# A transformer block with a depthwise convolution on one core: load order, where the residual sums are kept, an unpadded ring of pixels, and another folded tap

## The chip, the cores and the metric

The kernel runs on one core of a Trainium2 chip. The metric is the device time of one execution in microseconds; three runs of the kernel before gave 4190.55, 4192.3 and 4199.95 us, so the median is 4192.3 us.

The core's engines work side by side, each through its own queue in order: TensorE (PE) multiplies matrices, VectorE (DVE) and ScalarE (ACT) work element by element, GpSimd (POOL) does small arithmetic and issues the DMAs that add to their destination, SyncE (SP) issues plain loads and stores. Sixteen DMA engines carry all transfers.

## The reference

The input x has 16 images of 128 channels and 96 x 96 pixels, all float32. Per image the block computes, with every weight an input:

```python
xn1 = layernorm(x)                       # over the 128 channels of a pixel
q, k, v = xn1 @ wq.T, xn1 @ wk.T, xn1 @ wv.T   # 8 heads of 16 channels
attn = softmax(l2norm(q) l2norm(k)^T * 16**-0.5)   # 16 x 16 per head: sums over all 9216 pixels
x = x + (attn v) @ wp.T
xn2 = layernorm(x)
h1 = w_in xn2                            # 128 -> 512 channels
h2 = depthwise 3x3 convolution of h1, zero padding
x = x + w_out gelu(h2)                   # 512 -> 128 channels
```

The attention mixes channels, not pixels, so that per image it comes down to one 128 x 128 matrix and a bias (`mats`), which need the Gram matrix of all normalised pixels of that image.

## The kernel before, in words

**Tiling.** An image is cut into 8 bands of 12 rows (`BR`), a band into 3 units of 4 rows (`UR`, 384 pixels). Channels lie on the 128 partitions. There are 128 bands in all.

**First pass, norm a.** A band of x is loaded (L547). PE transposes 128 pixels at a time (L610), DVE takes mean and variance (L617), POOL computes the variance plus epsilon (L624) and its power -1/2 (L628), ACT scales the transposed pixels (L664), PE adds them to the Gram matrix (L678) and transposes them back (L715), and ACT copies them into the padded pixel tiles `xn` (L721).

**Attention.** Some twenty short steps on several engines turn the Gram matrix into `mats` (L779 to L875).

**Second pass, norm b.** PE multiplies a unit of normalised pixels by `mats` (L567). Either DVE adds the result to the x that is still in SBUF (L573; image 0, its first `XB_BUFS` = 6 bands), or ACT writes it with the bias into a buffer `xb` (L576) and a DMA of POOL adds x from DRAM (L579). The sum stays in that buffer. It is normalised as before (L610, L617, L624, L628, L632, L668, L715) and ACT writes the result over the same place of `xn` (L719), with a row more to the neighbouring part at a part's edge (L725).

**FFN.** The 512 hidden channels are 4 chunks. A *job* is one chunk of one band on the vector path: PE computes the hidden rows from `xn` (L900), ACT copies them to a padded buffer `h1` (L905), and two of 14 rows are kept for the next band by a copy of ACT (`halo`, L896). The tap at the corner, number 0, is folded into the hidden weights (`units`, L487), so that its product is the hidden value itself. Of the other eight taps DVE does six (L918, each multiplies and adds 1152 values per partition). ACT does two as products (L913), and two DMAs of POOL add them, one product to the other and the sum to `h3` (L922). ACT takes the GELU (L926). Chunk 3 of 62 of the 128 bands goes through PE instead: nine matmuls a unit with `w_in` and the tap multiplied together (`comp`, L968), and ACT's GELU (L974). That makes 450 jobs. PE multiplies `h3` by `w_out` (L991), ACT copies the result out (L1003), a DMA of POOL adds it to `xb` in SBUF (L1006), and SP stores `xb` to the output (L1010). In the last two bands DVE does that addition (L998).

**Pixels.** `xn` is six tiles of 24 rows with a row above and below and a zero column between rows (97 values a row); `window` takes shifted views of them. POOL zeroes the outer rows anew for each image (L407).

**Order.** Nothing is ordered by hand. `Plan` (L56) takes every operation with its engine, an assumed duration, a place (a job's number plus the offset of its kind in `AT`), what it reads and writes, and the pools of buffers; it then plays the engines through in time, each taking its ready operation with the lowest place, and the program is written in that order. Engines then run their queues in order and wait by semaphores. The assumed durations (`T_VARIANCE`, `T_POWER`, `T_ADD`, `t_dve`, ...) and `AT` therefore decide what stands behind what.

Of the kernel before, what the change touches and what calls it, by code (L numbers as in the profile page):

```python
# [26 lines left out]
THIRD, THIRD_OF, THIRD_CHUNK = (), 3, 1  # L27
PART, Z_PARTS = 24, 6
QT, QB = 4, 1
H_BANKS = 4  # L30
X1_BUFS, XB_BUFS, PR_BUFS, H3_BUFS, ZT_BUFS = 2, 6, 5, 10, 3
ADD_OF, ADD_BY_DMA = 1, (0,)
IN_TURN = ("tr", "h3", "pr", "xb", "x1")
AT = dict(
    load_w=10.25, weights=-46.8, zeros=-149.95, load_a=-129.7, forth_a=-2.85, stats_a=-6.55, variance_a=297.7,
    power_a=264.8, scaled_a=76.85, gram=-0.15, back_a=-106.5, place_a=51.75, attention=-125.2, mix=-20.25,
    residual=220.6, mixed=-149.95, add_x=-343.4, forth_b=0.85, stats_b=-219.5, variance_b=53.7, power_b=-244.15,
    shift_b=-78.6, scaled_b=4.05, back_b=-14.85, place_b=-112.4, evicted=4.9, add_out=-1.85, halo=191.1,
    hidden=2.75, kept=2.7, products=1, add_last=-73.7, tap=9.7, add_first=-58.05, gelu=173.1, conv=2.7,
    conv_gelu=8.75, out=6.1, add=-35.75, store=139.7, mix_0=-63.25, residual_0=414.1, mixed_0=-164.45,  # L40
    add_x_0=-281.3, gram_0=-43.8, forth_a_0=-74.3, forth_b_0=1.05, stats_a_0=-30.2, stats_b_0=-254.35,
    scaled_a_0=-88.5, scaled_b_0=171.2, back_a_0=-144.35, back_b_0=-18.9, place_a_0=-142.05, place_b_0=49.7,
    shift_b_0=-116.3, late=-68.9,
)
STEP = dict(scaled=0.3, hidden=0.1, products=0.5, tap=0.166, conv=1.6, conv_tap=0.03, out=0.8, out_part=0.05)
SLACK = 300
# [3 lines left out]
T_WEIGHTS = 12000  # L50
T_VARIANCE = 420
T_POWER = 1000
T_ADD, T_MOVE = 3100, 1800


class Plan:  # L56
# [7 lines left out]
    def __init__(self, **pools):  # L64
        self.free = {p: list(range(n)) for p, n in pools.items()}
        self.slot = {}
        self.ops, self.writer, self.readers, self.users = [], {}, {}, {}
        self.dma = 0.0
        self.two = 0.0

    def op(self, engine, ns, place, work, reads, writes, result, own=None, dma=0, two=False):
# [27 lines left out]
        self.ops.append((engine, ns, place, work, list(needs), new, result, own or result, dma, two))  # L99

    def order(self):
# [38 lines left out]
        def dispatch(engine, time):  # L140
# [19 lines left out]
            if o[8]:  # L160
                self.dma = max(time + ns + WAIT[engine], self.dma) + o[8]
                result = own = self.dma + result - time
            elif engine == "POOL":
                rest = self.two - time
                ns, result = (ns, result) if rest <= 0 else (rest + ns - 143, rest + result - 143)
                own = result
            if o[9]:
                self.two = time + ns + 35
# [42 lines left out]
def tile_restormer_block(  # L211
# [35 lines left out]
    UPP, PARTS = PART // UR, H // PART  # L247
    D = C // HEADS
    assert PE_CHUNK == NCH - 1 and BR * W >= 8 * P and QT % 2 == 0 and NU * TPU % (QB * QT) == 0 and C == P and UT % P == 0 and H % PART == 0 and PART % BR == 0 and NCH == 4
# [11 lines left out]

    xbs, x1s = {}, {}
# [12 lines left out]
    def column(v, name):  # L275
        t = const.tile([P, 1], F32, name=name)
        nc.scalar.dma_start(out=t, in_=v.rearrange("(c o) -> c o", o=1))
        return t

    w1, b1 = column(ln1_w, "w1"), column(ln1_b, "b1")  # L280
    w2, b2 = column(ln2_w, "w2"), column(ln2_b, "b2")

    wv_sb = const.tile([P, P], F32, name="wv_sb")
    nc.scalar.dma_start(out=wv_sb, in_=wv)
# [4 lines left out]
    nc.scalar.dma_start(out=dw, in_=w_dw.rearrange("(n p) o kh kw -> p n (o kh kw)", p=P))  # L289

# [13 lines left out]
    xns = [pad.tile([P, (PART + 2) * WP + 2], F32, name=f"xn{k}") for k in range(Z_PARTS)]  # L304
# [21 lines left out]
    def part_of(i, r):  # L326

        return (i * PARTS + r // PART) % Z_PARTS, r % PART

    def interior(i, u):  # L330
        k, r = part_of(i, u * UR)
        return window(xns[k], r + 1, UR, 1)

    def z_unit(i, u):
        k, r = part_of(i, u * UR)
        return ("z", k, r // UR)
# [8 lines left out]
    grams, mats, h3s, staged, outs = {}, {}, {}, {}, {}  # L345
# [12 lines left out]
    def z_units(k, r0, r1):  # L358

        return [("z", k, u) for u in range((r0 + UR - 1) // UR - 1, (r1 - 2) // UR + 1)]  # L360

# [4 lines left out]
    def t_dve(n):  # L366
        return 100 + 1.067 * n

    def t_act(n, scalars=0):
        return 95 + 93 * scalars + 0.832 * n  # L370

    def t_copy(n):
        return 40 + 0.832 * n
# [4 lines left out]
    def dve(ns, p, f, r, w, two=False):  # L378
        op("DVE", ns, p, f, r, w, ns + 120 + SLACK, ns + 120, two=two)

# [9 lines left out]
    def zeros(p):  # L390


        def around(t, r):
            nc.gpsimd.memset(t[:, : r * WP].rearrange("p (r w) -> p r w", w=WP)[:, :, :1], 0.0)
            nc.gpsimd.memset(t[:, r * WP :], 0.0)
# [3 lines left out]
        for t, r in [(t, PART + 2) for t in xns[:PARTS]] + [(t, BR + 2) for t in h1s] + [(t, PART + 2) for t in xns[PARTS:]]:  # L399
            op("POOL", 1000, at("zeros", p), lambda t=t, r=r: around(t, r), [], [("w", "in")], 1200)  # L400

    def ends(p, i):

        for r, at_, u in ((0, 0, -1), (H - 1, PART + 1, UPP)):
            k = part_of(i, r)[0]
            row = window(xns[k], at_, 1, 1)
            op("POOL", 400, at("zeros", p), lambda row=row: nc.gpsimd.memset(row, 0.0), [], [("z", k, u)], 600)  # L407

    def weights(p):

        mine = [("h3", ("weights", k)) for k in range(2)]
        v, names = staged, iter(range(99))

        def loads():
            a, b = (h3p.tile([P, BR * W], F32, tag="h3", name=f"weights_{k}") for k in range(2))
            v["win"] = a[:, :HID].rearrange("p (n c) -> p n c", c=P)
            v["wout"], v["wp"] = a[:, HID : 2 * HID], a[:, 2 * HID : 2 * HID + P]
            v["wqk"], v["wqkT"] = b[:, : 2 * P], b[:, 2 * P : 4 * P]
            v["wt"] = b[:, 4 * P : 8 * P].rearrange("p (t c) -> p t c", c=P)
            v["centre"], v["w1centre"], v["wvT"] = b[:, 8 * P : 9 * P], b[:, :P], b[:, P : 2 * P]  # L420
            nc.scalar.dma_start(out=v["wqk"][:, :P], in_=wq)
            nc.scalar.dma_start(out=v["wqk"][:, P:], in_=wk)
            nc.scalar.dma_start(out=v["wp"], in_=wp)
            nc.scalar.dma_start(out=v["win"], in_=w_in.rearrange("(n p) c kh kw -> p n (c kh kw)", p=P))
            nc.scalar.dma_start(out=v["wout"], in_=w_out.rearrange("c j kh kw -> c (j kh kw)"))

        def transposed(kind, parts, kept, gives):
# [10 lines left out]
            pe(440, at(kind, p), forth, mine, [h])  # L438
# [46 lines left out]
        def units():  # L485

            w0 = dw[:, :, 0]  # L487
# [12 lines left out]
        op("ACT", 400, at("load_w", p), loads, [], mine, T_WEIGHTS, dma=2 * T_MOVE)  # L500
        dve(1400, at("weights", p), units, [], [("w", "in")])
        dve(400, at("weights", p), shifts, [], [("w", "in"), ("w", "conv"), ("w", "shift")])
        transposed(
            "weights", lambda: [v["wqk"][:, :P], v["wqk"][:, P:], v["wp"], wv_sb], keep_qkp, ["qk"]
# [29 lines left out]
    def x_key(i, b, second):  # L534

        return "xb" if second or i == 0 and b < XB_BUFS else "x1"
# [14 lines left out]
    def norm(i, second, place_of):  # L551
# [8 lines left out]
        def x2(s, u):  # L560
# [19 lines left out]

            pm = ("h", (name, u))
            ins = [z_unit(i, u), ("m", i)]
            if loaded:
                pe(t_mm(UT), at("mix", s, i), mix, [*ins, xtok(u)], [pm])
                dve(t_dve(UT), at("residual", s, i), residual, [pm], [xtok(u)])
                return
            pe(t_mm(UT), at("mix", s, i), mix, ins, [pm, xtok(u)])
            act(t_act(UT, 1) - 43, at("mixed", s, i), mixed, [pm], [xtok(u)])
            if u % UPB == UPB - 1:
                xb = [xtok(b * UPB + k) for k in range(UPB)]  # L590
                add(at("add_x", s, i), add_x, [], xb)

        def pixels(s, m):
# [88 lines left out]

            trs, bt = [(key_, (name, q)) for q in qs], ("batch", (name, m))
# [5 lines left out]
            op("POOL", T_VARIANCE, at("variance" + ab, s), variance, [], [bt], T_VARIANCE + 33 + SLACK)  # L689
            op("POOL", T_POWER, at("power" + ab, s), power, [], [bt], T_POWER + 33 + SLACK)  # L690
# [16 lines left out]
        def channels(s, u):  # L707
# [15 lines left out]
            def place_row(k, r, row):  # L723
                to = window(xns[k], r, 1, 1)
                nc.scalar.activation(to, rows(d["pB"])[:, row : row + 1, :], AF.Identity, bias=b2)  # L725

            copies = []
            if second and u % UPP == 0 and u > 0:
                copies.append((part_of(i, u * UR - 1)[0], PART + 1, 0, UPP))
            if second and u % UPP == UPP - 1 and u < NU - 1:  # L730
                copies.append((part_of(i, (u + 1) * UR)[0], 0, UR - 1, -1))

# [4 lines left out]
            for k, r, row, of in copies:  # L737
                act(225, at("place" + ab, s, i), lambda k=k, r=r, row=row: place_row(k, r, row), [pb, ("w", "shift")], [("z", k, of)])


        for u in range(0, NU if not second else 0, UPB):
            load(at("load_a", place_of(u * TPU)), i, u // UPB)
# [139 lines left out]
    def conv_job(j, g, n):  # L882

        i, b = divmod(g, NB)
        kz, r0 = part_of(i, b * BR)
# [204 lines left out]
```

## Time and profile before

| what | before |
|---|---|
| runs | 4190.55, 4192.3, 4199.95 us |
| span of the profiled execution, first to last instruction | 4197.8 us (2.15 us under the slowest of the runs, 5.5 us over their median) |
| PE busy | 4120.2 us (98%) |
| DVE busy | 4089.8 us (97%) |
| ACT busy | 3697.8 us (88%) |
| POOL busy | 2606.6 us (62%) |
| bytes moved by DMA | 831.16 MB, mean 198 GB/s |
| DMA queue of POOL (adds) / of SP (loads, stores) | 83.3% / 9.8% of the 16 engines' time |

Busy times are of the instructions as recorded, which overlap at their ends: for the pace of an engine that works without a gap, the distance from one start to the next is read from the chain of waits. A row of the windows gives, for a stretch of time, each engine's busy microseconds and, at its end, the granted clock of PE, the share of the DMA engines' time and the GB/s. A row of the groups gives line, engine, operation, output and inputs, count, busy time, mean ns of one, and after the bar the engine's idle time just before them and what ended it.

### The profile page before, as it was taken

How to read it: one execution, taken by the hardware profiler on the slowest of the kernel's cores; microseconds unless marked ns; L12 is line 12 of the kernel's file. 1: busy time of each engine (PE TensorE's matmuls, PEld its weight loads, DVE VectorE, ACT ScalarE, POOL GpSimd, SP SyncE). 2: the span in 40 equal slices, each digit the busy share in tenths (PEclk: the TensorE clock that was granted, in tenths of full speed). 3: DMA queues.
4: the chain of work that ended last, by engine and by line, in shares of the span. 5: the costliest groups of instructions: out<-in, count | busy, mean ns of one | idle time of the engine just before them, and what ended most of it. 6: DMA issues, size and time to landing. Idle time of an engine off the chain costs nothing.

```text
span 4197.8 us, 52159 instructions
## 1 busy us (share of the span) xinstructions
PE 4120.2 (98%) x17265; PEld 2648.1 (63%) x17265; DVE 4089.8 (97%) x4450; ACT 3697.8 (88%) x7232; POOL 2606.6 (62%) x2397
## 2 busy tenths in 40 slices
PE   8999999999999999999999999999999999999999
PEld 6666666666666666656666666666666666665555
DVE  6999999999999999999999999999999999999998
ACT  5899988999899888889899989998899888999885
POOL 4757666565666757767576565666656666675442
PEclk9999999999999999999999999999999999999999
DMA  3899999999999999999999999999999999999997
GB/s 91 178 195 213 194 215 196 198 203 204 205 206 202 209 193 205 198 211 202 195 210 205 204 203 199 210 199 210 200 204 208 194 212 200 201 203 191 196 190 167
DMA packets 204797, 831.16 MB, mean 198 GB/s; under 512 B 23664, under 2 KB 25072, under 8 KB 204528
## 3 DMA queue, kind: packets, MB, share of 16 engines
q0 software_dynamic: 165024, 676.01, 83.3%
q1 hardware_dynamic: 37152, 151.01, 9.8%
q8 instruction: 137, 2.24, 0.2%
q10 hardware_dynamic: 2352, 0.81, 0.1%
q14 instruction: 132, 1.08, 0.1%
HBM read 148.26 MB, written 75.50 MB: 53 GB/s over the span
## 4 chain that ended last, share of the span: by engine, by line
PE 59%; DVE 27%; ACT 5%; POOL 4%; DMA 2%; issue 2%; ACTq 0%; POOLq 0%; DVEq 0%
DVE h L918 24%; PE h L968 16%; PE h L991 15%; PE h L900 12%; PE g L678 4%; PE h L567 4%; PE pB_a L715 2%; PE pT_b L610 2%; PE pB_b L715 2%; PE pT_a L610 2%; DVE st_a L617 1%; DMA h<-pr 1%; DVE st_b L617 1%; ACT pr L913 1%; POOL rstd_b L628 1%
## 5 line engine op out<-in xcount | busy, mean ns | idle before, releaser
L918 DVE SCALAR_TENSOR_TENSOR h<-h,ratio,h 128x1152 f32<-128x1152 f32 x2252 | 3105.2, 1403 | 4.1
L913 ACT ACTIVATE pr<-h,ratio 128x1152 f32<-128x1152 f32 x898 | 1159.8, 1296 | 44.0 <-DMA h<-pr 29.8
L968 PE MATMUL h<-xn,comp 128*128 128x384 f32 x3348 | 1195.2, 486 | 2.5 <-ACT h L905 2.5
L991 PE MATMUL h<-h,woutT 128*128 128x384 f32 x3072 | 1138.7, 488 | 5.8 <-ACT h L926 2.8
L900 PE MATMUL h<-xn,winT 128*128 128x384 f32 (+1 forms) x2700 | 1073.2, 502 | 6.1 <-ACT h L905 3.4
L968 PEld LDWEIGHTS h<-xn,comp 128*128 128x128 f32 x3348 | 609.1, 190 | 369.0 <-issue 8.1
L991 PEld LDWEIGHTS h<-h,woutT 128*128 128x128 f32 x3072 | 559.6, 190 | 351.8 <-issue 11.6
L905 ACT COPY h<-h 128x384 f32<-128x384 f32 (+1 forms) x1350 | 667.5, 527 | 116.5 <-PE h L900 89.0
L922 POOL DMA_DIRECT2D h<-pr x449 | 436.4, 972 | 468.2 <-DVE h L918 140.2
L922 POOL DMA_DIRECT2D pr<-pr x449 | 441.9, 984 | 406.2 <-ACT pr L913 368.9
L900 PEld LDWEIGHTS h<-xn,winT 128*128 128x128 f32 x2700 | 480.7, 190 | 292.8 <-issue 45.1
L918 DVE SCALAR_TENSOR_TENSOR h<-h,ratio 128x1152 f32<-128x1152 f32 x450 | 631.1, 1407 | 11.9 <-PE h L991 5.3
L926 ACT ACTIVATE h<-h 128x1152 f32<-128x1152 f32 x452 | 545.3, 1209 | 13.8 <-DMA h<-pr 10.5
L628 POOL TENSOR_TENSOR rstd_a<-ve_a,mhalf 128x4 f32<-128x4 f32 x288 | 539.7, 1875 | 12.7
L628 POOL TENSOR_TENSOR rstd_b<-ve_b,mhalf 128x4 f32<-128x4 f32 x288 | 535.3, 1859 | 12.2
L624 POOL TENSOR_SCALAR ve_a<-st_a 128x4 f32<-128x4 f32 x288 | 340.9, 1184 | 260.9 <-DVE st_a L617 254.0
L668 ACT ACTIVATE zT<-pT_b,nb_b,rstd_b 128x128 f32<-128x128 f32 x1132 | 432.8, 488 | 33.3 <-DVE nb_b L632 30.2
L624 POOL TENSOR_SCALAR ve_b<-st_b 128x4 f32<-128x4 f32 x288 | 325.8, 1131 | 194.5 <-DVE st_b L617 188.8
L664 ACT ACTIVATE zT<-pT_a,rstd_a 128x128 f32<-128x128 f32 x1080 | 317.3, 409 | 44.8 <-POOL rstd_a L628 43.0
L678 PEld LDWEIGHTS g<-zT 128*128 128x128 f32 x2304 | 296.5, 192 | 51.0 <-issue 4.3
L678 PE MATMUL g<-zT 128*128 128x129 f32 x2304 | 306.5, 276 | 0.0
L567 PE MATMUL h<-xn,mwT 128*128 128x384 f32 x768 | 294.1, 496 | 11.7 <-ACT h L905 6.6
(175 smaller groups left out, 3710.6 us busy)
## 6 DMA issues: line engine op xcount, KB each, us to landing
pr<-pr POOLq DMA_DIRECT2D x449, 576.0 KB, 7.0
h<-pr POOLq DMA_DIRECT2D x449, 576.0 KB, 7.1
x<-in_x_dram SPq DMA_DIRECT2D x128, 576.0 KB, 6.4
out_dram<-x SPq DMA_DIRECT2D x127, 576.0 KB, 7.0
x<-out POOLq DMA_DIRECT2D x126, 576.0 KB, 7.4
x<-in_x_dram POOLq DMA_DIRECT2D x122, 576.0 KB, 7.2
out_dram<-x SPq DMA_DIRECT2D x3, 192.0 KB, 1.9
weights<-in_L_conv_w_in_dram ACTq DMA_DIRECT2D x1, 256.0 KB, 2.7
```

Source lines behind the costliest of these rows:

```text
L567: nc.tensor.matmul(rows(pm), lhsT=mats[i][0], rhs=interior(i, u), start=True, stop=True)
L624: nc.gpsimd.tensor_scalar(ve, d["mv"][:, :, 2], 1.0 / C, EPS, ALU.mult, ALU.add)
L628: nc.gpsimd.tensor_tensor(rstd, d["ve"], mhalf, ALU.pow)
L678: nc.tensor.matmul(grams[i][:, : P + 1], lhsT=zt[:, :P], rhs=zt, start=(q == 0 and k == 0), stop=(q == NU * TPU // QT - 1 and k == QT - 1),)
L900: nc.tensor.matmul(rows(ph), lhsT=winT[:, n, :], rhs=window(xn, r0 + r, e - r, 1), start=True, stop=True)
L905: nc.scalar.copy(window(h1_, r, e - r, 1), rows(d.pop(("ph", r))))
L913: nc.scalar.activation(to, shifted(t), AF.Copy, scale=ratio[:, n, t : t + 1])
L918: nc.vector.scalar_tensor_tensor(h3, shifted(t), ratio[:, n, t : t + 1], onto, ALU.mult, ALU.add)
L922: nc.gpsimd.dma_start(out=to, in_=d["pr", t], accum_op=ALU.add)
L926: nc.scalar.activation(h3, h3, AF.Gelu)
L968: nc.tensor.matmul(d["pc"], lhsT=comp[:, t, :], rhs=window(xn, r0 + dy, UR, dx), start=(t == 0), stop=(t == 8),)
L991: nc.tensor.matmul(rows(d["po"]), lhsT=woutT[:, n, :], rhs=h3s[g, n][:, s * UR : (s + 1) * UR, :], start=(k == 0), stop=(k == NCH - 1),)
```

## The change

- **Start.** ACT first runs one small exponential (which loads that table), then issues the weights' loads in two groups, those of the attention and those of the FFN, instead of some small ones at once and the rest later. The steps that make tap ratios and shifts (`units`, `shifts`) get the place of the late weight steps and read from the second group. Three bands of image 0 (`X0_BUFS`), not six, have their x kept for DVE's addition.
- **Residual sums.** When a band's x plus attention is complete, SP stores it to the output at once (`keep_x2`), which frees the buffer after the norm has read it. The FFN's result is later added by POOL's DMA to the output in DRAM, after a wait on that store. The last two bands stay as they were.
- **Pixels.** One ring of 144 rows of 96 values without padding replaces the six tiles. `pieces` gives a range of rows, in two parts where it crosses the ring's end. There are no zero rows to write, no rows written twice, and the matmuls of `comp` leave out rows and columns that lie outside the image. Only `h1` keeps its zero columns.
- **Taps.** Tap 4, the centre, is folded. DVE does taps 3, 0, 2, 5, 6, 8, the first over full rows and the other five over 95 of 96 columns; ACT and DMA do 1 and 7. In the first and the last band of an image, taps that reach over the edge leave out that row, and the hidden row outside the image is not computed.
- **Shares and buffers.** 61 instead of 62 bands have chunk 3 on PE, so 451 jobs. x1 buffers 2 to 3, xb 6 to 3, h3 10 to 12.
- **Plan.** New offsets in `AT`, own offsets for image 0 in more kinds, other assumed durations; the assumption that POOL's small operations wait for DVE's taps is gone, their assumed durations are longer instead.

```diff
+RING = 144
-PE_BANDS = (0, 2, 4, 6, 8, 10, 12)
-PE_OF = 15
-PE_LAST = (0, 1, 2, 4, 5, 7)
+PE_SHARE = (7, 15)
+PE_LAST = (0, 1, 2, 4, 5)
-DMA_TAPS = (1, 2, 3)
+DMA_TAPS = (1, 7)
+DVE_TAPS = (3, 0, 2, 5, 6, 8)
+CENTRE = 4
-X1_BUFS, XB_BUFS, PR_BUFS, H3_BUFS, ZT_BUFS = 2, 6, 5, 10, 3
+X1_BUFS, XB_BUFS, PR_BUFS, H3_BUFS, ZT_BUFS = 3, 3, 5, 12, 3
+X0_BUFS = 3
-SLACK = 300
+SLACK = 200
-T_VARIANCE = 420
-T_POWER = 1000
-T_ADD, T_MOVE = 3100, 1800
+T_VARIANCE = 1150
+T_POWER = 1870
+T_ADD, T_MOVE = 254 * BR, 133 * BR
...
-    xns = [pad.tile([P, (PART + 2) * WP + 2], F32, name=f"xn{k}") for k in range(Z_PARTS)]
+    ring = pad.tile([P, RING, W], F32, name="xn")
+    def pieces(i, r, n):
+        out, done = [], 0
+        while done < n:
+            at_ = (i * H + r + done) % RING
+            m = min(n - done, RING - at_)
+            out.append((done, m, ring[:, at_ : at_ + m, :]))
+            done += m
+        return out
...
+        op("ACT", 1400, at("tables", p), table, [], [tables], 1500)
+        op("ACT", 2700, at("load_1", p), loads_1, [], [mine[1], small_1], T_WEIGHTS, dma=1000)
+        op("ACT", 2300, at("load_2", p), loads_2, [], [mine[0], small_2], T_WEIGHTS, dma=1800)
+        dve(1400, at("late", p), units, [small_2], [("w", "in")])
...
+            def keep_x2():
+                done = nc.sync.dma_start(out=ov[i, :, b * BR * W : (b + 1) * BR * W], in_=xbs[i, b])
+                stores[i * NB + b] = done.ins
...
         def tap(t):
             h3 = h3_of(g, n)
-            onto = shifted(0) if t == left[0] else h3
-            nc.vector.scalar_tensor_tensor(h3, shifted(t), ratio[:, n, t : t + 1], onto, ALU.mult, ALU.add)
+            o0, o1 = reach(t)
+            w0, w1 = (0, W) if t == left[0] else (t % 3 == 0, W - (t % 3 == 2))
+            onto = shifted(CENTRE, o0, o1) if t == left[0] else h3[:, o0:o1, w0:w1]
+            nc.vector.scalar_tensor_tensor(
+                h3[:, o0:o1, w0:w1], shifted(t, o0, o1, w0, w1), ratio[:, n, t : t + 1], onto, ALU.mult, ALU.add
+            )
...
         def add_out():
-            nc.gpsimd.dma_start(out=xbs[i, b], in_=outs[g].rearrange("p r w -> p (r w)"), accum_op=ALU.add)
+            to = ov[i, :, b * BR * W : (b + 1) * BR * W]
+            done = nc.gpsimd.dma_start(out=to, in_=outs[g].rearrange("p r w -> p (r w)"), accum_op=ALU.add)
+            tc.add_manual_dep(
+                done.ins, stores.pop(g).name, mybir.DependencyInfo(mybir.DependencyClass.Sync, mybir.DependencyReason.DATA),
+                reason="adds to what was stored",
+            )
```

More of the change, by code (lines that the diff above doesn't have):

```diff
@@ L33 @@
+X0_BUFS = 3
+LAST_ADDS = 2
 IN_TURN = ("tr", "h3", "pr", "xb", "x1")
 AT = dict(
[L35 to L43, printed above, removed]
+    load_1=-81.8, load_2=-81.05, tables=-300.65, weights=-241.6, zeros=-79.35, load_a=-132.3, forth_a=-3.95,
@@ new lines @@
+    stats_a=-119.7, variance_a=57.65, power_a=43.15, scaled_a=67.75, gram=-0.3, back_a=-131.9, place_a=-4.05,
+    attention=-126.85, mix=-6.1, residual=-100.05, mixed=-72.7, add_x=-106.2, forth_b=-1.2, stats_b=-57.55,
+    variance_b=-94.65, power_b=108.15, shift_b=-68.05, scaled_b=71.3, back_b=-38.35, place_b=67.85, evicted=4.6,
+    add_out=-80.65, halo=139.4, hidden=2.8, kept=-53.4, products=2.05, add_last=-216.85, tap=8.1,
+    add_first=-80.7, gelu=650.75, conv=2.7, conv_gelu=7.9, out=6.35, add=107.4, store=112.35, mix_0=-6.7,
@@ L98, in op @@
         needs.pop(k, None)
[L99 removed]
+        self.ops.append((engine, ns, place, work, list(needs), new, result, own or result, dma))
     def order(self):
```

246 lines of the change are left out of this document (126 added, 120 removed).

## The prediction

> **What bounds the kernel now.** I read the page's head and its chain first, then four long windows, then the chain in order of time, to learn which engine is full and at what pace.
>
> ```profile
> PE 4120.2 (98%) x17265; PEld 2648.1 (63%) x17265; DVE 4089.8 (97%) x4450; ACT 3697.8 (88%) x7232; POOL 2606.6 (62%) x2397
> PE 59%; DVE 27%; ACT 5%; POOL 4%; DMA 2%; issue 2%; ACTq 0%; POOLq 0%; DVEq 0%
> ...
> 0.00:120.00 120.00, 104.67 (x640) 83.24 (x641) 84.49 (x213) 67.58 (x168) 54.02 (x129) 0.99 0.37 102
> 120.00:1000.00 880.00, 859.54 (x3634) 552.04 (x3634) 865.59 (x931) 790.63 (x1558) 569.83 (x504) 0.99 0.95 200
> 1000.00:2000.00 1000.00, 984.60 (x4145) 631.91 (x4144) 985.83 (x1054) 900.15 (x1772) 657.08 (x573) 1.00 0.96 203
> 2000.00:3000.00 1000.00, 989.53 (x4175) 637.06 (x4174) 989.52 (x1059) 908.15 (x1781) 638.55 (x576) 1.00 0.97 204
> 3000.00:4000.00 1000.00, 987.67 (x4031) 628.26 (x4030) 983.97 (x1039) 894.46 (x1728) 620.11 (x553) 0.99 0.96 201
> 4000.00:4100.00 100.00, 100.00 (x351) 60.49 (x350) 94.73 (x91) 82.43 (x145) 44.12 (x43) 1.00 0.92 192
> ...
> 523.49 15.94 DVE h L918 x12
> 1227.59 5.81 PE h L968 x18
> ```
>
> The chain changes between PE and DVE, and the windows say why: from 120 to 4000 us DVE is idle for 14.4 + 14.2 + 10.5 + 16.0 = 55 us of 3880 and PE for 20.5 + 15.4 + 10.5 + 12.3 = 59. Two engines are full at once, and the DMA engines, at 0.95 to 0.97 of their time, are nearly so. Only work taken from both PE and DVE shortens the span, and DMA must not grow. At the start (0 to 120) DVE idles 35.5 us and PE 15.3. The last two rows give the true pace without overlap: a tap 15.94 / 12 = 1.328 us, a matmul pass over 384 columns 5.81 / 18 = 0.323 us, so 0.841 ns a column.
>
> **The change part by part.** The sum is made against the profiled span of 4197.8 us, and the difference applied to the median of the runs, 4192.3, which lies 5.5 under that span.
>
> ```profile
> L918 DVE SCALAR_TENSOR_TENSOR h<-h,ratio,h 128x1152 f32<-128x1152 f32 x2252 | 3105.2, 1403 | 4.1
> L968 PE MATMUL h<-xn,comp 128*128 128x384 f32 x3348 | 1195.2, 486 | 2.5 <-ACT h L905 2.5
> L900 PE MATMUL h<-xn,winT 128*128 128x384 f32 (+1 forms) x2700 | 1073.2, 502 | 6.1 <-ACT h L905 3.4 <-ACT out L1003 2.4
> L918 DVE SCALAR_TENSOR_TENSOR h<-h,ratio 128x1152 f32<-128x1152 f32 x450 | 631.1, 1407 | 11.9 <-PE h L991 5.3 <-ACT h L905 4.8 <-ACT zT L668 1.6
> L725 ACT ACTIVATE xn<-pB_b,b 128x96 f32<-128x96 f32 x96 | 36.0, 375 | 0.0
> L573 DVE SCALAR_TENSOR_TENSOR x<-h,d,x 128x384 f32<-128x384 f32 x18 | 11.0, 616 | 3.1 <-PE h L567 3.0
> L407 POOL MEMSET xn<- 128x96 f32 x32 | 9.2, 290 | 24.9 <-PE h L968 15.9 <-PE h L900 9.1
> ```
>
> *Taps on DVE.* Before, 2252 + 450 = 2702 taps of 1152 values: 3,112,704. After, 451 jobs have 6, and the last one 2 more: 2708 taps. Five taps a job lose 12 values (a column over 12 rows): 27,060 in all. 57 jobs in first bands and 56 in last ones lose a row of 95 in two taps each, and the final job one row of 96: 21,566. That leaves 3,070,990, so 41,714 fewer. The price of a value is the slope between two rows of this instruction, (1403 - 616) / (1152 - 384) = 1.025 ns: -42.7 us. Six more instructions cost their constant, 1328 - 1152 x 1.025 = 147 ns: +0.9. Nine of the 18 additions at L573 go: -5.5. DVE: **-47.3 us**. [...]
>
> *Matmuls.* `comp` had 62 x 27 products of 384 columns, two passes each (the 3348): 642,816 columns. After: 61 bands, less one column over four rows in 6 of 9 taps (61 x 3 x 6 x 4 = 4,392), less three cut rows in each of 15 edge bands (15 x 286 = 4,290): 623,766. The hidden rows fall by 115 (one a job in first and last bands, two in each of 8 chunk-3 jobs that now take a halo, 14 more for the 451st job): 11,040 columns. So 30,090 columns by 2 passes by 0.841 ns: PE **-50.6 us**. The ring's seams cut a few matmuls in two; that happens in every third image, in one place, and costs under 1 us.
>
> *ACT and POOL.* The 96 edge rows of L725 (36.0 us) and 115 copied rows go, 8 halo copies and 9 `mixed` units come; the 32 memsets at L407 (9.2 us, before which POOL stood for 24.9) go. ACT is idle 12% of the time and POOL 38%, so I count nothing; were this cover gone, some 35 us on ACT and 34 on POOL would be gains.
>
> *DMA.* The prices follow from these rows.
>
> ```profile
> span 4197.8 us, 52159 instructions
> q0 software_dynamic: 165024, 676.01, 83.3%
> q1 hardware_dynamic: 37152, 151.01, 9.8%
> ...
> pr<-pr POOLq DMA_DIRECT2D x449, 576.0 KB, 7.0
> h<-pr POOLq DMA_DIRECT2D x449, 576.0 KB, 7.1
> x<-in_x_dram SPq DMA_DIRECT2D x128, 576.0 KB, 6.4
> out_dram<-x SPq DMA_DIRECT2D x127, 576.0 KB, 7.0
> x<-out POOLq DMA_DIRECT2D x126, 576.0 KB, 7.4
> x<-in_x_dram POOLq DMA_DIRECT2D x122, 576.0 KB, 7.2
> ```
>
> The four kinds of adds are 1146 and take 83.3% of 4197.8 us: 3.05 us of all 16 engines each. Loads and stores are 256 and take 9.8%: 1.61 us. After, 900 product adds, of which 112 are a row shorter (-9.3), 125 additions of x and 126 to the output make 1141.7, so -4.3 adds, -13 us; plain transfers stay 256. What an add *into DRAM* costs is in no row. From below: x added from DRAM lands after 7.2 us where SBUF adds land after 7.0 to 7.4, so a DRAM side may cost nothing. From above: an add and a store's whole pass, 3.05 + 1.61, that is +1.61 x 126 = 203 us. I take nothing extra, since the 7.2 row is the nearest: it too is an add with DRAM on one side. A gain below nothing is excluded, because the same bytes are read and written. [...]
>
> DMA work from 120 to 4100 us is 836 + 960 + 970 + 960 + 92 = 3818 us (shares by lengths). After, 3805 in 3980 - 47 = 3933: a share of 0.967. Still hidden, but no longer looser than DVE or PE by more than 2%.
>
> *Waits added and moved.* The stores of x plus attention stand in SP's queue ahead of the next image's loads, behind a landing of 7.2 us (longest 12.5):
>
> ```profile
> SPq L1010 <- DMA x<-out: 2145.7, 117, 47.4
> SPq L547 <- PE pT_a L610: 1633.6, 103, 34.0
> ...
> PEld pT_a L610: 0.5, 1
> PE pT_a L610: 0.3, 1
> ...
> DMA to landing us min/median/max: 5.7/7.2/12.5
> ```
>
> SP already waits as long before its stores, and loads wait for x1 buffers; what norm a waited for loads is in the third and fourth rows, 0.8 us in all; the third x1 buffer gives each load a band (4197.8 / 128 = 32.8 us) more, which covers the 12.5. Without that cover PE's transposes of norm a would be late by up to 12.5 us a band. POOL's output add now also waits for that store, issued bands earlier, so for nothing; were it late, products and the variance steps of POOL would stand behind it. A band's `xb` is now held from its first mixed unit to the last transpose: 32.8 + 1.0 + 7.2 + 32.8 = 74 us of the 98 that three buffers give.
>
> *Start.* Here these rows count (the last from the windows of 10 us).
>
> ```profile
> 5.51 3.65 PE L610 MATMUL h<-ident,x 128*128 128x128 f32 x16 [5.51 <-DMA x<-in_x_dram]
> 7.86 0.17 DVE L488 TENSOR_SCALAR unit<-dw 128x4 f32<-128x4 f32 x1 [6.80 <-DMA dw<-in_L_conv_w_dw_dram]
> 10.26 2.74 DVE L617 BATCH_NORM_STATS2 st_a<-h 128x6 f32<-128x256 f32 x8
> 21.73 0.35 ACTq L421 DMA_DIRECT2D weights<-in_L_conv_wq_dram  x1
> 24.14 0.62 ACT L664 ACTIVATE zT<-h,rstd_a 128x128 f32<-128x128 f32 x2 [1.93 <-DMA weights<-in_L_conv_wk_dram]
> ...
> 0.00:10.00 10.00, 3.65 (x16) 3.28 (x16) 2.04 (x14) 0.00 (x0) 2.35 (x34) 1.00 0.78 228
> ```
>
> DVE's first statistics wait until 10.26 behind small weight steps, though x has been there since 5.5; and ACT issues weight loads from 21.73 to 24.14 amid the scaling. Both go: up to 4.0 + 2.4 us. Against that, 0.79 MB of weights (four matrices of 64 KB, two of 256 KB) now share the DMA engines with the first bands of x, 3.4 us at the 228 GB/s of the first 10 us. I take **-4 us** (0 to -6.4).
>
> *Order.* Nearly every offset in `AT` is new, which no row prices. The 55 us that DVE idles between 120 and 4000 may vanish or double. I leave them as they are.
>
> Sum: the smaller of DVE's and PE's cuts, -47.3, and -4 at the start: 4192.3 - 51.3 = **4141 us**.
>
> **The rivals.**
>
> *DMA becomes the bound because adds into DRAM are dear (slower).* At +1.61 us per add the DMA work of the middle is 3805 + 203 = 4008 us. Even at a share of 1.0 that is longer than the 3980 us now: 4192.3 + 28 - 4 = 4216 us. It decides from 0.44 us per add (56 us) if 0.97, the highest of the thousand-us rows, is the ceiling, or 1.39 us (175 us) if 1.0 is. Against it stands the 7.2 row. [...]
>
> *DMA is the ceiling already.* If the middle cannot go above 0.97 and a DRAM add costs the 0.2 us by which landings scatter (25 us), 3830 / 0.97 = 3948: -32 - 4, 4156 us; at 0.35 us it is 4176. For: all three resources are within 2% of each other. Against: DMA releases only 2% of the chain.
>
> *The order is worse.* With three `xb` for six, mixing or the second norm comes late and DVE or PE stand. 24 us of slack in 98 must be eaten first; then 0.4 us a band (51 / 128) cancels the gain, and 0.6 gives 4192.3 + 77 - 51 = 4218 us. For: every wait in the steady part now runs through a shorter ring of buffers. Against: 24 us is twice the longest landing.
>
> *The narrow taps save nothing.* If a row of 95 costs as much as one of 96, 27,060 x 1.025 = 28 us of DVE's cut go: 4169 us. Against: the form with both inputs in rows takes 1407 ns, the other 1403.
>
> *The order is better.* The new assumed durations fit these rows, the old ones (420 and 1000 ns) did not:
>
> ```profile
> L628 POOL TENSOR_TENSOR rstd_a<-ve_a,mhalf 128x4 f32<-128x4 f32 x288 | 539.7, 1875 | 12.7
> L624 POOL TENSOR_SCALAR ve_a<-st_a 128x4 f32<-128x4 f32 x288 | 340.9, 1184 | 260.9 <-DVE st_a L617 254.0
> ```
>
> If half of DVE's 55 us of idle time goes, 4141 - 28 = 4113 us.
>
> **How the numbers follow.** About 0.2% (8 us) can be told from no change here. Chances: forecast 0.48 (4115 to 4168), better order 0.14, DMA ceiling 0.11, worse order 0.10, dear adds 0.09, narrow taps 0.08. Faster: 0.48 + 0.14 + 0.08 and 0.08 of the ceiling, 0.78. Within 0.2%: 0.03 of the ceiling, 0.04 of the worse order. Slower: the rest, 0.15. The range from 4095 to 4205 leaves out the dear adds, half of the worse order and a third of the better one.
>
> **What would show it.** DVE busy some 47 us lower with 2708 taps, the five narrow ones about 13 ns under the wide; L968's and L900's successors together 51 us lower in pace; 61 bands by matmul; the add into DRAM landing near 7.4 us; q0's time about 13 us less; DMA share in the middle 0.96 to 0.98; the first statistics near 6.5 us. Wrong would be the forecast if q0's time grows by over 50 us, if idle time of DVE named for DMA, `xb` or `nb` rises well above 55 us, or if POOL or SP wait long for a store.

## The result, and the profile after

| what | before | changed |
|---|---|---|
| median of the runs, us | 4194.66 | 4147.07 (4139.83 to 4156.64) |
| ratio | 1 | 0.9889, 95% interval 0.9871 to 0.9907 |
| span of the profiled execution, us | 4197.8 | 4145.3 |

The change takes 47.6 us; 51.3 were forecast. (The median before is here of four runs, the fourth 4197.01 us.) The page's head, DMA queues, chain and DMA issues of the changed kernel:

```profile
span 4145.3 us, 52245 instructions
PE 4060.7 (98%) x17287; PEld 2654.1 (64%) x17287; DVE 4040.2 (97%) x4446; ACT 3656.0 (88%) x7158; POOL 2602.5 (63%) x2358
...
q0 software_dynamic: 165744, 673.46, 84.9%
q1 hardware_dynamic: 37152, 151.01, 9.9%
...
PE 63%; DVE 24%; ACT 5%; DMA 4%; POOL 3%; issue 2%; POOLq 0%; ACTq 0%; DVEq 0%
...
h<-pr POOLq DMA_DIRECT2D x450, 576.0 KB, 8.4
out_dram<-out POOLq DMA_DIRECT2D x126, 576.0 KB, 7.7
x<-in_x_dram POOLq DMA_DIRECT2D x125, 576.0 KB, 8.5
```

DVE is busy 4089.8 - 4040.2 = 49.6 us less, and its idle time is almost what it was (4197.8 - 4089.8 = 108.0 us before, 4145.3 - 4040.2 = 105.1 after). POOL's queue of adds took more of the DMA engines, not less: 0.833 x 4197.8 = 3497 us before, 0.849 x 4145.3 = 3519 now.

Where DVE's idle time lies is read from the same windows as before (the last two numbers of a row are DMA share and GB/s):

```profile
0.00:120.00 120.00, 105.73 (x642) 84.12 (x643) 91.22 (x216) 76.50 (x183) 58.65 (x119) 0.99 0.57 153
120.00:1000.00 880.00, 865.28 (x3727) 567.18 (x3726) 866.06 (x948) 793.43 (x1571) 577.29 (x508) 1.00 0.96 202
1000.00:2000.00 1000.00, 984.93 (x4233) 644.88 (x4232) 982.80 (x1061) 899.18 (x1767) 651.80 (x571) 1.00 0.98 204
2000.00:3000.00 1000.00, 992.17 (x4242) 649.04 (x4241) 990.17 (x1067) 907.28 (x1784) 651.20 (x574) 1.00 0.98 206
3000.00:4000.00 1000.00, 970.82 (x3986) 623.94 (x3985) 976.35 (x1043) 884.67 (x1705) 619.36 (x542) 0.99 0.95 199
```

In the first 120 us DVE does 91.22 us of work instead of 84.49. From 120 to 4000 it is idle for 64.6 us, 9.5 more than before. That second number scatters: in the profile of the changed kernel's second execution (span 4136.5 us, below) it is 55.9. The DMA engines now work at 0.95 to 0.98.

The taps of the changed kernel in the groups, by form:

```profile
L929 DVE SCALAR_TENSOR_TENSOR h<-h,ratio,h 128x1140 f32<-128x1140 f32 x2029 | 2772.2, 1393 | 0.9
L929 DVE SCALAR_TENSOR_TENSOR h<-h,ratio 128x1152 f32<-128x1152 f32 x451 | 632.8, 1409 | 6.7 <-ACT h L908 6.6
```

The first tap in order of time (start, duration), in the changed kernel:

```profile
82.99 1.44 DVE L929 SCALAR_TENSOR_TENSOR h<-h,ratio 128x1152 f32<-128x1152 f32 x1 [2.82 <-ACT h L908]
```

and in the kernel before:

```profile
94.95 1.42 DVE L918 SCALAR_TENSOR_TENSOR h<-h,ratio 128x1152 f32<-128x1152 f32 x1 [2.48 <-ACT h L905]
```

The narrow tap takes 16 ns less than the wide one of the same execution (the form with both inputs in rows was 4 ns over the other before, so 12 are the column's, as 12 values should be at the 1.025 ns of the prediction's slope). The first tap comes 12.0 us earlier. ACT's first table load (1.28 us) starts at 0.79 us instead of 13.71.

### The profile page after: what moved, and what is told of

It reads as the page before. It is cut to its first block, busy times and chain, and to the rows that moved or that the text cites. A ratio compares the mean times of both kernels' runs of the same rounds, so it can differ in the third digit from the quotient of the medians.

```text
span 4145.3 us, 52245 instructions
## 1 busy us (share of the span) xinstructions
PE 4060.7 (98%) x17287; PEld 2654.1 (64%) x17287; DVE 4040.2 (97%) x4446; ACT 3656.0 (88%) x7158; POOL 2602.5 (63%) x2358
## 4 chain that ended last, share of the span: by engine, by line
PE 63%; DVE 24%; ACT 5%; DMA 4%; POOL 3%; issue 2%; POOLq 0%; ACTq 0%; DVEq 0%
DVE h L929 21%; PE h L994 17%; PE h L1018 16%; PE h L905 13%; PE g L692 4%; PE h L572 4%; PE pB_a L730 2%; PE pT_b L624 2%; PE pT_a L624 2%; PE pB_b L730 2%; DMA h<-pr 2%; DVE st_b L631 1%; DVE st_a L631 1%; ACT pr L922 1%; DMA pr<-pr 1%
## 5 line engine op out<-in xcount | busy, mean ns | idle before, releaser
L929 DVE SCALAR_TENSOR_TENSOR h<-h,ratio,h 128x1140 f32<-128x1140 f32 (+1 forms) x2257 | 3056.8, 1383 | 1.1
L922 ACT ACTIVATE pr<-h,ratio 128x1152 f32<-128x1152 f32 (+1 forms) x900 | 1153.2, 1286 | 100.6 <-DMA h<-pr 52.8
L994 PE MATMUL h<-xn,comp 128*128 128x380 f32 (+3 forms) x3324 | 1166.9, 481 | 9.2 <-ACT h L908 5.7
L1018 PE MATMUL h<-h,woutT 128*128 128x384 f32 x3072 | 1113.8, 488 | 10.8 <-ACT h L908 6.9
L905 PE MATMUL h<-xn,winT 128*128 128x384 f32 (+3 forms) x2746 | 1052.5, 490 | 15.7 <-ACT x L581 8.2
L994 PEld LDWEIGHTS h<-xn,comp 128*128 128x128 f32 x3324 | 604.4, 191 | 355.2 <-ACT h L908 8.6
L908 ACT COPY h<-h 128x384 f32<-128x384 f32 (+2 forms) x1353 | 657.0, 521 | 73.5 <-PE h L905 53.7
L936 POOL DMA_DIRECT2D pr<-pr x450 | 427.7, 950 | 435.0 <-ACT pr L922 387.0
L936 POOL DMA_DIRECT2D h<-pr x450 | 454.2, 1009 | 368.2 <-DVE h L929 153.0
L905 PEld LDWEIGHTS h<-xn,winT 128*128 128x128 f32 x2746 | 491.2, 190 | 301.8 <-issue 29.4
L642 POOL TENSOR_TENSOR rstd_a<-ve_a,mhalf 128x4 f32<-128x4 f32 x288 | 551.0, 1913 | 15.0
L642 POOL TENSOR_TENSOR rstd_b<-ve_b,mhalf 128x4 f32<-128x4 f32 x288 | 531.0, 1845 | 10.9
L572 PE MATMUL h<-xn,mwT 128*128 128x384 f32 x768 | 310.3, 490 | 7.5 <-ACT h L908 4.3
```

Of the source, the lines that this page charges most:

```text
L572: nc.tensor.matmul(rows(pm), lhsT=mats[i][0], rhs=interior(i, u), start=True, stop=True)
L642: nc.gpsimd.tensor_tensor(rstd, d["ve"], mhalf, ALU.pow)
L905: nc.tensor.matmul(rows(ph)[:, k : k + m, :], lhsT=winT[:, n, :], rhs=z, start=True, stop=True)
L908: nc.scalar.copy(window(h1_, r, e - r, 1), rows(d.pop(("ph", r))))
L922: nc.scalar.activation(d["pr", t][:, o0:o1, :], shifted(t, o0, o1), AF.Copy, scale=ratio[:, n, t : t + 1])
L929: nc.vector.scalar_tensor_tensor(h3[:, o0:o1, w0:w1], shifted(t, o0, o1, w0, w1), ratio[:, n, t : t + 1], onto, ALU.mult, ALU.add)
```

## The experiments

Three questions were open. How much of work taken from an engine becomes time? Are the DMA engines, or the adds into DRAM, a limit? What do the start and the order of the program bring? Where an experiment says "in its own order", only the work of an operation was changed, not what the planner is told of it. The executions come in three groups, each with runs of the kernel before beside it. The kernel before took 4191.48, 4207.92 and 4190.65 us there, the last two on a chip of the same number, so between groups ratios to it are compared. Of the three, only the first has runs of the changed kernel.

### How much of an engine's work becomes time

The changed kernel again:

> The changed kernel again, as the base of the three runs beside it. All theories: 0.989 of the kernel before, 4139 to 4157 us.

4141.34 us, ratio 0.9881 (0.9868 to 0.9895). It is the base of the next three.

All DVE taps over 96 columns:

```diff
-            w0, w1 = (0, W) if t == left[0] else (t % 3 == 0, W - (t % 3 == 2))
+            w0, w1 = 0, W
```

> The changed kernel in its own order, with the five narrow taps of each job over all 96 columns again (451 x 60 = 27,060 values more, at 1.025 ns: DVE busy 28 us more, nothing else). Theory A (DVE and PE are both full and the span follows either of them locally): 10 to 28 us longer than the changed kernel. Theory B (the DMA engines are by now the ceiling): within 5 us of it. Theory C (narrow rows save nothing on DVE): no difference, and DVE's busy time the same.

More work for PE:

```diff
+            if t == order[0] and s == 0:
+                nc.tensor.matmul(d["pc"][:, :3, :], lhsT=comp[:, t, :], rhs=got[0][2][:, :3, :], start=True, stop=True)
```

> The changed kernel in its own order, with one matmul over 288 columns more in the first unit of each of the 61 bands on PE, whose result the next matmul overwrites: 61 x 2 passes x 288 x 0.841 = 29.5 us more for PE, nothing else. Theory A: 10 to 29 us longer than the changed kernel. Theory B: within 5 us. If only DVE is the bound: within 5 us.

Both edits:

> Both additions together: DVE 28 us and PE 29.5 us more. Theory A: 25 to 35 us longer than the changed kernel, less than the sum of the two alone if each alone is near 28, more than either if each alone is near half. Theory B: under 10 us.

| kernel | us | ratio | busy PE / DVE, us | against the base, us |
|---|---|---|---|---|
| changed | 4141.34 | 0.9881 (0.9868 to 0.9895) | 4056.7 / 4040.6 | |
| full taps | 4154.88 | 0.9917 (0.9903 to 0.993) | 4067.1 / 4064.0 | +13.5 |
| more for PE | 4148.23 | 0.9901 (0.9888 to 0.9915) | 4080.8 / 4044.2 | +6.9 |
| both | 4160.77 | 0.993 (0.9917 to 0.9943) | 4087.0 / 4067.1 | +19.4 |

The chains of the changed kernel's second execution, with full taps, and with more for PE, one fence each:

```profile
PE 70%; DVE 18%; ACT 5%; DMA 3%; POOL 2%; issue 1%; POOLq 0%; ACTq 0%; DVEq 0%
```

```profile
PE 61%; DVE 25%; ACT 5%; DMA 4%; POOL 3%; issue 2%; POOLq 0%; ACTq 0%; DVEq 0%
```

```profile
PE 78%; DVE 9%; ACT 6%; DMA 4%; POOL 2%; issue 1%; POOLq 0%; ACTq 0%; DVEq 0%
```

28 us of DVE's work cost 13.5 us, 29.5 us of PE's work 6.9, and the two together 19.4, about their sum. The second is small: its interval touches that of the base, though its fastest execution (4144.79 us) lies above the slowest of the base (4143.79). The expectations had at least 10 us for PE and at least 25 for both, so these two came out under them. The time follows neither engine in full, and each alone counts. As slopes, 13.5 / 28 = 0.48 for DVE and 6.9 / 29.5 = 0.23 for PE, together 0.7. These are divided by the planned loads; the busy times rose less, by 23.4 us on DVE and 24.1 on PE, and by them the slopes are 0.58 and 0.29. Each difference is uncertain by some 8 us, as two intervals are in it.

That the two engines are the bound in different stretches is my reading and is not shown in full. The chains fit it where PE is loaded: PE's share is 63% and 70% in the two executions of the changed kernel and 78% with more for PE. With full taps DVE has 25%, hardly more than the 24% of the changed kernel's first execution.

The rival "narrow rows save nothing" falls: DVE's busy time rose by 23.4 us when the columns were put back. The tap's row in the changed kernel's second execution and with full taps, one fence each:

```profile
L929 DVE SCALAR_TENSOR_TENSOR h<-h,ratio,h 128x1140 f32<-128x1140 f32 x2029 | 2772.3, 1392 | 0.9
```

```profile
L929 DVE SCALAR_TENSOR_TENSOR h<-h,ratio,h 128x1152 f32<-128x1152 f32 x2030 | 2797.7, 1404 | 0.9
```

The same from the other side, the new taps in the kernel before:

```diff
-DMA_TAPS = (1, 2, 3)
+DMA_TAPS = (1, 7)
+DVE_TAPS = (3, 0, 2, 5, 6, 8)
+CENTRE = 4
-            w0 = dw[:, :, 0]
+            w0 = dw[:, :, CENTRE]
-            onto = shifted(0) if t == left[0] else h3
-            nc.vector.scalar_tensor_tensor(h3, shifted(t), ratio[:, n, t : t + 1], onto, ALU.mult, ALU.add)
+            first = t == left[0]
+            o0, o1 = (1 if b == 0 and t // 3 == 0 else 0), (BR - 1 if b == NB - 1 and t // 3 == 2 else BR)
+            w0, w1 = (0, W) if first else (t % 3 == 0, W - (t % 3 == 2))
+            onto = shifted(CENTRE)[:, o0:o1, :] if first else h3[:, o0:o1, w0:w1]
+            nc.vector.scalar_tensor_tensor(
+                h3[:, o0:o1, w0:w1], shifted(t)[:, o0:o1, w0:w1], ratio[:, n, t : t + 1], onto, ALU.mult, ALU.add
+            )
```

> The kernel before, in its own order, with the changed kernel's taps on DVE alone (centre folded, five taps over 95 columns, edge rows left out): 450 x 60 + 21,376 = 48,400 values fewer for DVE, 49 us of its busy time, nothing else. If the span follows DVE at the 0.48 that the full taps showed (13.5 us for 28): 24 us shorter than before, ratio 0.994. If in full, as the prediction had it: 49 us, ratio 0.988. If DMA is the ceiling: under 5 us.

4183.61 us beside 4207.92, ratio 0.9947 (0.9933 to 0.9962): -0.53%, 22 us of 4192, where the slope had forecast 24 and the full pass-through 49. The expectation calls the 49 us the prediction's, but the prediction's own words, that only work taken from both engines shortens the span, would give nothing here. DVE's busy time fell by 42.0 us (4089.8 to 4047.8 in the profiles), short of the 49; so 22 us is 0.45 of the planned cut and 0.53 of the recorded one. The page's head and chain:

```profile
PE 4112.9 (98%) x17265; PEld 2647.4 (63%) x17265; DVE 4047.8 (97%) x4450; ACT 3698.7 (88%) x7232; POOL 2579.1 (62%) x2397
PE 78%; DVE 10%; ACT 6%; POOL 2%; DMA 2%; issue 1%; ACTq 0%; POOLq 0%; DVEq 0%
```

With DVE relieved alone, PE's share rises from 59% to 78% (it is 66% in the run with the tap ratios computed later, below, which takes as long as the kernel before). This one part of the change brings nearly half of its gain.

### The DMA engines

Without the 126 adds to the output:

```diff
-            to = ov[i, :, b * BR * W : (b + 1) * BR * W]
-            done = nc.gpsimd.dma_start(out=to, in_=outs[g].rearrange("p r w -> p (r w)"), accum_op=ALU.add)
-            tc.add_manual_dep(
...
+            stores.pop(g)
```

> The changed kernel in its own order without the 126 DMAs that add the FFN's result to the output: the stored sums stay as the output of those bands, so part of the computation is left out. It takes 126 x 3.40 = 429 us of the DMA engines away (a tenth of their work) and nothing else but 126 issues of POOL. Theory A (PE and DVE set the time, and their waits on DMA are the 83 us that ACT's products stand and little beside): 5 to 25 us shorter than the changed kernel's 4141. Theory B (DMA is the ceiling of the middle): 40 us shorter or more.

And with the adds into a spare tile of SBUF:

```diff
+    spare = const.tile([P, BR * W], F32, name="spare")
+    nc.vector.memset(spare, 0.0)
...
-            done = nc.gpsimd.dma_start(out=to, in_=outs[g].rearrange("p r w -> p (r w)"), accum_op=ALU.add)
+            nc.gpsimd.dma_start(out=spare, in_=outs[g].rearrange("p r w -> p (r w)"), accum_op=ALU.add)
```

> The changed kernel in its own order, but each of those adds goes to one spare tile in SBUF instead of the output, so the FFN is left out of the result of 126 bands. Only the destination changes. A price of DRAM as read from the packets (3.40 us an add against 3.02 before): 126 x 0.38 = 48 us of the DMA engines less. Theory A: 0 to 6 us shorter than the changed kernel. Theory B: 20 to 48 us shorter.

Without the adds the ratio is 0.9856 (0.9837 to 0.9876), 0.0025 or 10 us under the changed kernel's 0.9881, with intervals that overlap a little. The windows show how far the load fell:

```profile
1000.00:2000.00 1000.00, 986.75 (x4239) 647.15 (x4237) 985.26 (x1061) 904.40 (x1773) 638.36 (x541) 1.00 0.88 186
2000.00:3000.00 1000.00, 988.36 (x4215) 646.93 (x4214) 982.78 (x1066) 904.39 (x1773) 647.44 (x543) 1.00 0.88 186
```

The DMA share falls from 0.97 or 0.98 to 0.88 and PE and DVE are as full as they were. A tenth of all DMA work is worth about 10 us, by the ends of the two intervals at most 24 (0.9895 - 0.9837 = 0.0058), where 40 or more were expected of a ceiling. The DMA engines are not the ceiling. Even the 10 us may come by way of the buffers: ACT's products stood 25.8 us for POOL's adds to `h3`, against 52.8 and 43.9 in the two executions of the changed kernel.

With the adds in SBUF the ratio is 0.9898 (0.9881 to 0.9914): no gain from the cheaper destination, if anything a loss within the intervals, for which I have no cause. What the destination costs the DMA engines is in the row of POOL's queue, of this kernel (span 4170.4 us)

```profile
q0 software_dynamic: 165744, 673.46, 83.8%
```

and of the changed kernel's second execution (span 4136.5 us):

```profile
q0 software_dynamic: 165744, 673.46, 85.1%
```

0.838 x 4170.4 = 3495 us against 0.851 x 4136.5 = 3520: 25 us for 126 adds, 0.20 us each, about half of the 48 us expected. It costs no time that these runs can show. Without the adds (span 4146.9 us) the same row is

```profile
q0 software_dynamic: 147600, 599.13, 75.2%
```

0.752 x 4146.9 = 3118 us, so 402 us less than the changed kernel's 3520, where 429 were expected: 3.19 us an add.

### The start and the order

The start of the change in the kernel before, which needed other buffers and so an order planned anew:

```diff
-X1_BUFS, XB_BUFS, PR_BUFS, H3_BUFS, ZT_BUFS = 2, 6, 5, 10, 3
+X1_BUFS, XB_BUFS, PR_BUFS, H3_BUFS, ZT_BUFS = 2, 5, 5, 11, 3
-        op("ACT", 400, at("load_w", p), loads, [], mine, T_WEIGHTS, dma=2 * T_MOVE)
-        dve(1400, at("weights", p), units, [], [("w", "in")])
+        op("ACT", 1400, at("tables", p), table, [], [tables], 1500)
+        op("ACT", 2700, at("load_1", p), loads_1, [], [mine[1], small_1], T_WEIGHTS, dma=1000)
+        op("ACT", 2300, at("load_2", p), loads_2, [], [mine[0], small_2], T_WEIGHTS, dma=1800)
+        dve(1400, at("late", p), units, [small_2], [("w", "in")])
...
```

> The kernel before with the start of the changed one alone (table first, the weights' loads in two early groups, the tap ratios among the late steps; 11 h3 and 5 xb buffers, as 10 h3 do not suffice for it). If the start gives what the first tap shows (82.99 against 94.95 us): 7 to 12 us shorter than before, ratio 0.997 to 0.998. If my forecast of 4 us for it was right: ratio 0.999. The whole order of the program is planned anew, so some microseconds either way may come from that.

A miss: 4275.2 us, ratio 1.0166 (1.0144 to 1.0187), 1.7% slower. Its first tap is early enough, but what follows is not. Its windows:

```profile
0.00:120.00 120.00, 104.59 (x626) 81.27 (x627) 85.55 (x210) 65.72 (x164) 53.43 (x127) 0.99 0.40 106
120.00:1000.00 880.00, 854.02 (x3615) 544.89 (x3614) 860.83 (x919) 784.85 (x1549) 555.85 (x502) 1.00 0.94 199
...
3000.00:4000.00 1000.00, 965.67 (x3966) 610.81 (x3965) 952.39 (x1013) 873.04 (x1699) 583.17 (x546) 0.99 0.92 194
```

Its first tap in order of time:

```profile
90.89 1.42 DVE L930 SCALAR_TENSOR_TENSOR h<-h,ratio 128x1152 f32<-128x1152 f32 x1 [2.98 <-ACT h L917]
```

And a row of its waits (total us, times, longest):

```profile
DVE h L930 <- ACT h L917: 46.8, 24, 5.3
```

The first tap is 4.1 us earlier than before, a third of the 12.0; what brings the rest (buffers, offsets, the ring) was not separated. Nearly all of the loss lies in the steady part: from 120 to 4000 us DVE is idle for 122.1 us (55.1 before), and the last row says that its taps stood 46.8 us for hidden rows (4.8 before). As I read it, the order is bad because the offsets were made for another set of buffers; buffers and order changed together here. So this run says nothing against the start, and shows that a program planned anew with one buffer more and one less can lose 70 us.

A start earlier in the kernel's own order:

```diff
         def unit_parts():
+            units()
+            shifts()
...
-        dve(1400, at("weights", p), units, [], [("w", "in")])
+        dve(1400, at("weights", p), lambda: None, [], [("w", "in")])
...
```

> The kernel before in its own order, with the tap ratios and shifts computed on DVE just ahead of the late weight step instead of first of all. The first statistics start near 6.3 us instead of 10.26. If an earlier start carries through: 2 to 4 us shorter, ratio 0.999. If the start is set by PE's pace from 30 us on: no difference.

```profile
6.75 0.43 DVE L619 BATCH_NORM_STATS2 st_a<-h 128x6 f32<-128x256 f32 x1 [5.71 <-PE h L612]
...
91.95 1.42 DVE L920 SCALAR_TENSOR_TENSOR h<-h,ratio 128x1152 f32<-128x1152 f32 x1 [2.48 <-ACT h L907]
```

The statistics start 3.5 us earlier and the first tap 3.0, but the ratio is 1.0001 (0.999 to 1.0013), 4190.54 us. A gain of 3 us cannot be excluded, one of 5 can. Inconclusive.

Neighbouring orders, of the changed kernel:

```diff
-SLACK = 200
+SLACK = 220
```

> The changed kernel with one number of its planner changed, SLACK from 200 to 220 ns, so that the same operations, buffers and offsets are put into another order by a tenth of the assumed wait. If the order matters only through the amounts of work: 0.988 to 0.990 of the kernel before, as the changed kernel. If an order is worth tens of microseconds by itself (the start alone, planned anew, came out 70 us slower): 5 to 60 us off, and longer rather than shorter.

and of the kernel before:

```diff
-SLACK = 300
+SLACK = 320
```

> The same for the kernel before: SLACK from 300 to 320 ns. If its order is no better than a neighbour's: ratio 0.998 to 1.002. If its offsets fit one order closely: 1.003 to 1.015.

The changed kernel's neighbour has a ratio of 0.9871 (0.9857 to 0.9885), 4133.57 us: no worse, and no better beyond the intervals. The neighbour of the kernel before is 0.44% slower (1.0044, 1.003 to 1.0057), 18 us. A re-ordering by a fifteenth of an assumed wait (20 of 300 ns) can thus move the time by 18 us, more than the 4 us at which the whole start was priced and nearly as much as the 22 of the taps.

The planner's assumed durations, in the changed kernel set back to the old ones:

```diff
-SLACK = 200
+SLACK = 300
-T_VARIANCE = 1150
-T_POWER = 1870
-T_ADD, T_MOVE = 254 * BR, 133 * BR
+T_VARIANCE = 420
+T_POWER = 1000
+T_ADD, T_MOVE = 3100, 1800
-        return 103 + 1.067 * n
+        return 100 + 1.067 * n
-        return 105 + 93 * scalars + 0.832 * n
+        return 95 + 93 * scalars + 0.832 * n
-        return 50 + 0.832 * n
+        return 40 + 0.832 * n
```

> The changed kernel planned with the assumed durations of the kernel before (420 and 1000 ns for POOL's two steps of the norm, SLACK 300, the older constants for DVE, ACT and DMA), everything else as changed. If the new durations make a better order (the rival of the prediction): 15 to 60 us longer than the changed kernel, with the waits of POOL's variance steps and of ACT's scaling for them grown. If order does not matter: 0.988 to 0.990.

4273.86 us, ratio 1.0205 (1.0189 to 1.022): 133 us over the changed kernel's 4141.34, with the same count of instructions on every engine. The waits of this kernel (total us, times, longest):

```profile
POOL ve_a L638 <- DVE st_a L631: 376.5, 179, 12.1
POOL ve_b L638 <- DVE st_b L631: 357.0, 160, 9.1
ACT zT L678 <- POOL rstd_a L642: 159.4, 115, 8.0
DVE nb_b L646 <- POOL rstd_b L642: 136.0, 160, 2.9
```

and the last two of the changed kernel:

```profile
ACT zT L678 <- POOL rstd_a L642: 22.8, 16, 8.1
DVE nb_b L646 <- POOL rstd_b L642: 9.0, 9, 2.0
```

DVE's idle time grew from 105.1 us to 4271.5 - 4064.7 = 206.8, and its wait for the power alone by 127. As I read it, the planner put DVE's `nb` and ACT's scaling where a power of 1000 ns would be ready; it takes 1845 to 1913 ns in the changed kernel, and both engines stand in front of their queues. Several numbers were set back together, so which of them does the harm was not separated. (The kernel before has the short durations too, but together with the assumption that POOL waits for taps, which this kernel has not; and the offsets were made for the new numbers.)

## Why the prediction was right, and where its terms were not

The time came out 6 us from the forecast and inside the likeliest case's own range. The mechanism held in the main: two full engines, work taken from both, and DMA traffic that stays hidden. Step by step:

- *DVE's work.* Forecast -47.3 us, measured -49.6 in the busy time. The counts, 2708 taps and 61 bands on PE, hold, and so does the price of a value: 12 values less are 12 ns less (1392 against 1404).
- *PE's work.* Forecast -50.6 us; the busy time fell by 59.5 (4120.2 to 4060.7), in which ends of instructions overlap. It also fell by 7.3 with the new taps alone, where PE's work is unchanged, so it does not measure the cut to some us. Added up from start to start, the passes of the two lines in question (L968 and L900 before, L994 and L905 after) come to about 50 us less, as forecast.
- *"The smaller of DVE's and PE's cuts."* The ground of this step failed: that only work taken from both engines shortens the span. 42 us from DVE alone gave 22 (16 to 28 by the interval). Whether the smaller cut counts in full when both are made is not settled: with both loads, 28 us more cost 19.4, and by the ends of the intervals 9 to 31. By the slopes on planned loads the cuts are worth 0.48 x 47.3 + 0.23 x 50.6 = 34 us, by those on recorded busy times 0.58 x 49.6 + 0.29 x 59.5 = 46.
- *The start, -4 us.* Undersized as an event: the first tap is 12.0 us earlier, and DVE has done 6.7 us more work by 120 us.
- *The sum.* So 14 or 2 of the 47.6 us are left, and the slopes are not known well enough to say which. The start's 6.7 to 12.0 may be in it, but no experiment showed it in the time: one could not resolve 3 us, the other was swamped by its order. Whether each step was right, or two errors of opposite signs met, stays open. DVE's account, 49.6 us less work, 6.7 less idle time up to 120 us, 9.5 more up to 4000 and 5.7 less after, gives the 52.5 between the two spans; but it must come out, and names no cause. That the total gain agrees to 4 us is luck in part, since the four runs of the changed kernel alone lie 17 us apart.
- *Adds into DRAM, "nothing extra".* 0.20 us each by the DMA queues (25 us in all), against the 0 I took and the 1.61 of the upper bound. POOL's queue grew by 22 us where I had -13; the other 10 of these 35 us no run explains. No cost in time was seen, as said.
- *DMA share 0.967 in the middle, "still hidden".* Measured 0.95 to 0.98, and a tenth less of it gives about 10 us. The rival that DMA is the ceiling, or becomes it, is refuted. I had kept 0.20 of the chance for the two, because 0.97 looked like a limit; 0.98 is reached while PE and DVE keep their pace.
- *Waits.* The add to the output did not stand for its store: its row in the groups shows 122.1 us of idle time before it, 101.2 of them for ACT's copy, and no store is among what is listed for the rest. SP waits 2496.7 us before its early stores (2145.7 before its stores in the kernel before); no engine waits for these stores, and the loads kept PE waiting once, for 5.2 us at the start. The add's row:

```profile
L1034 POOL DMA_DIRECT2D out_dram<-out x126 | 124.2, 986 | 122.1 <-ACT out L1030 101.2 <-ACT h L900 8.0 <-DVE h L929 4.0
```

- *Order.* "The order is better" got 0.14. It is not better by half of DVE's idle time (64.6 and 55.9 us in two executions, 55.1 before). What the runs add is how much worse an order can be: planned with the old durations against offsets made for the new ones, the same instructions take 3.2% longer, nearly three times the gain. That is the price of a mismatch and does not show that the new durations would beat the old ones with offsets of their own.

## What to carry to other kernels

When two engines are full, do not price a cut as all or nothing: load one engine a little in an otherwise unchanged order, and read the slope (0.48 and 0.23 here), with enough load and runs to tell it from the scatter. A resource at 0.98 of its time need not be a bound (the DMA engines here were none); take a tenth of its work away before calling it one. In a program whose order is planned from assumed durations, measure these and keep them true, and test one part of a change in a fixed order, or the re-planning will hide it.

## What the runs showed of the hardware

A DMA that adds 576 KB into DRAM cost the DMA engines only 0.20 us more than one that adds into SBUF (3520 against 3495 us of POOL's queue, 126 adds), 7% of the 3.05 us that an add of the kernel before took on average. It landed after 7.7 us; in the spare tile it was 7.0, but the products' adds within SBUF also came down there, from 7.4 to 7.1.

A tap with three operands in 12 rows of 95 took 12 ns less than one in 12 rows of 96 (1392 against 1404): at 1.025 ns a value that is its 12 values, and nothing is visible for the broken rows.

POOL's power of 128x4 values took 1.00 to 1.04 us up to 78 us in the changed kernel, 1.03 to 6.08 from 84 to 200 us, after DVE's first tap (82.99 us), with medians of 2.09 (`rstd_a`) and 2.07 (`rstd_b`), and 1.85 to 1.91 on average over the run. What makes it longer there is not shown. Two from before the first tap:

```profile
13.59 1.01 POOL L642 TENSOR_TENSOR rstd_a<-ve_a,mhalf 128x4 f32<-128x4 f32 x1
...
76.90 1.01 POOL L642 TENSOR_TENSOR rstd_b<-ve_b,mhalf 128x4 f32<-128x4 f32 x1
```

one after it:

```profile
98.26 2.09 POOL L642 TENSOR_TENSOR rstd_a<-ve_a,mhalf 128x4 f32<-128x4 f32 x1
```

and all of them in its groups:

```profile
L642 POOL TENSOR_TENSOR rstd_a<-ve_a,mhalf 128x4 f32<-128x4 f32 x288 | 551.0, 1913 | 15.0
L642 POOL TENSOR_TENSOR rstd_b<-ve_b,mhalf 128x4 f32<-128x4 f32 x288 | 531.0, 1845 | 10.9
```
